# A decoder layer in fp32 on one core: first tiles on two DMA queues, a TensorE start on the identity, and work moved between ScalarE, VectorE and GpSimd

## The chip, the core and the metric

The kernel runs on one core of one Trainium2 chip. The metric is device time in microseconds. The core has five engines that run beside each other and wait for each other on semaphores: TensorE (PE in the profile; its weight loads are PEld), VectorE (DVE), ScalarE (ACT), GpSimd (POOL) and SyncE (SP, which here only issues DMAs). Each engine works its own list of instructions in order.

## The reference

16 sequences of 256 rows with 256 columns go through one layer, all in fp32. Cut to what is computed:

```python
# 1: four heads over 256 fixed keys and values (w_fc, w_proj)
n = layernorm(x) * ln_g + ln_b
p = square(relu(n_heads @ k.T))            # heads of 64, no softmax
x = layernorm(x + (x + p @ v))
# 2: cross attention with 16 heads of 16 on ctx, biased by clipped differences
D = clip(frac[:, None, :] - frac[:, :, None], -0.2, 0.2)
a = gamma * (Q @ K.T) / 4 + delta * (ap * max(D, 0) + an * min(D, 0))
x = layernorm(x + softmax(a) @ V @ Wo.T + bo)
# 3: feed-forward, 1024 wide; each row takes the low-rank addition of one of 8 experts
e = argmax(x @ gate_W.T + gate_b)
x = layernorm(x + relu(x @ wi.T + wi_b + lora(x, e)) @ wo.T + wo_b)
```

## The kernel before

The 4096 rows are 8 blocks of 512 (four tiles of 128 rows) for steps 1 and 3, and 16 batches of 256 for step 2. The order of every engine's work is written out by hand; nothing is scheduled by a planner.

**Loading and the first block (L261 to L307, L896 to L901).** The four tiles of block 0 are loaded by four DMAs on SP (L263), each 128 x 256, and those of later blocks by one DMA each (L260). ln_g and ln_b (L70) and then vv, the values of step 1 (L84), are issued on ACT's queue, with a load of ACT's function tables between them (L78). The keys kT follow the tiles on SP (L83), then block 1, and, from the first slot of the loop, the weights of step 2 (L113). Block 0 is measured by VectorE (L189, L190, one tile after the other), its inverse deviation is made by ACT and VectorE (L198 to L209), and the normed rows xn by ACT (tiles 0 and 1, L249) and VectorE (tiles 2 and 3, L287). TensorE turns them with transposes against an identity (L295), ACT and VectorE evict the two halves (L299, L304).

**Stage 1 (L916 to L994)** is a loop over blocks with eight slots each. In a slot TensorE makes two scores (L314, into one of two PSUM buffers ps_a), ACT takes their Relu (L322), VectorE squares it (L324), and TensorE multiplies the previous slot's squares with vv (L334), into two banks, one of them tagged W. Everything else, such as the next block's norm, is hung into fixed slots.

**Stage 2 with 3 (L1014 to L1148)** is a loop over n = 0 to 65. Step n works on group n: four of the sixteen heads of batch n // 4. In each step TensorE makes the logits of group n (L609) on top of a positive bias that ACT has put into the four banks ps_l (`positive`, L600). The negative bias of the next group is made ahead: `negative(count)` (L582) lets POOL make `count` of its four parts (L588) and ACT the rest (L593). VectorE adds it and takes the row maxima (L624), and the maxima are subtracted for half of the heads by POOL and for half by VectorE (L639). The group before is turned by transposes (`turned`, L649), ACT takes the exponentials (L656), and the one before that is multiplied with the values (`attend`, L665). A "large piece" of another batch hangs in each step (`pieces`, L687): for n a multiple of 4 it is the next batch's queries (`queries`, L433; four products, L437, evicted with scale and bias by ACT, L447).

The feed-forward of a block lies in eight steps, counted by `tb, part = divmod(n - 15, 8)`: part 0 turns its rows (L749), part 1 makes the gates (L764, evicted by ACT, L772), part 2 routes (L777 to L809) and makes the first half of the inner product, part 3 the second half (`inner`, L817; `lora`, L838), and parts 4 to 7 the outer product of one tile each (`finish`, L876, with L860). So n = 16, 24, 32, 40, 48 and 56 have both queries and gates.

All these pieces take PSUM banks from `tile_b` (L49), which hands out three banks in turn: two of psB and the one tagged W. `tile_v` hands out one more, tagged V, which `attend` uses.

The last block of stage 1 (`rest`) has its second norm in stage 2: measured in n = 16 to 19, its scale made in n = 20, its four tiles scaled by ACT and given their bias by POOL (`norm_out`, L376 to L379) at the ends of n = 24, 25, 26 and 27 (L1141). They are batches 14 and 15.

**The end (L1150 to L1187)** finishes the last batch and the feed-forward of blocks 6 and 7. Block 6 makes its first inner half in the four banks ps_l, `lora(0)` evicts them, and its second half goes into the same four banks.

Of the kernel before, what the change touches and what calls it, by code (L numbers as in the profile page):

```python
# [9 lines left out]
FP = mybir.dt.float32  # L10
AF = mybir.ActivationFunctionType
ALU = mybir.AluOpType
AX = mybir.AxisListType

P = 128
EPS = 1e-5
CLAMP = 0.2
BIG = 3.0e38

# [2 lines left out]
def tile_decoder_layer(ctx: ExitStack, tc: tile.TileContext, a: dict, out: bass.AP):  # L22


    nc = tc.nc
    NTOK, C = a["x"].shape
    B, S = a["frac"].shape
    NT = NTOK // P
    NB = NTOK // 512
    CC = C // P  # L30
# [9 lines left out]
    const = ctx.enter_context(tc.tile_pool(name="const", bufs=1))  # L40
# [8 lines left out]
    def tile_b():  # L49

        if turns:
            turns[0] += 1
            if turns[0] % 3 == 0:
                return psV.tile([P, 512], FP, tag="W", name="ps_b")
        return psB.tile([P, 512], FP, tag="B", name="ps_b")

    def tile_v(tag="V"):
        return psV.tile([P, 512], FP, tag=tag, name="ps_v")


    ident = const.tile([P, P], FP, name="ident")
# [3 lines left out]
    rev = const.tile([P, 4, E], FP, name="rev")  # L65
    for e in range(E):
        nc.gpsimd.memset(rev[:, :, e : e + 1], float(E - e))
    def columns(name, src, eng):
        t = const.tile([P, src.shape[1]], FP, name=name)
        eng.dma_start(out=t, in_=src)  # L70
        return t


    kT = const.tile([P, 4, C], FP, name="kT")
    ln_g = columns("ln_g", a["ln_g"], nc.scalar)
    ln_b = columns("ln_b", a["ln_b"], nc.scalar)

    nc.scalar.preload_act_table_set("natural_log_exp_and_others")  # L78
    vv = const.tile([P, CC, C], FP, name="vv")

    def load_first():
        for h in range(2):
            nc.sync.dma_start(out=kT[64 * h : 64 * h + 64], in_=a["kT"])  # L83
        nc.scalar.dma_start(out=vv, in_=a["vv"].rearrange("(c p) f -> p c f", p=P))  # L84


    W = E + ER
    wq, wk, wv, wo = (const.tile([P, CC, C], FP, name=n) for n in ("wq", "wk", "wv", "wo"))
# [8 lines left out]
    bq_s = const.tile([P, CC], FP, name="bq_s")  # L97
# [4 lines left out]
    gamma, delta, qscale = (const.tile([P, 1], FP, name=n) for n in ("gamma", "delta", "qscale"))  # L102
    fcol, nfcol = (const.tile([P, NT], FP, name=n) for n in ("fcol", "nfcol"))
    wib = const.tile([P, FC], FP, name="wib")
# [4 lines left out]

    def load_cross():  # L110
        load = nc.sync.dma_start
        for t, n in ((wk, "wkT"), (wv, "wvT"), (wq, "wqT")):
            load(out=t, in_=a[n].rearrange("(c p) f -> p c f", p=P))  # L113
        for t, n in ((bq, "bq"), (bk, "bk"), (fcol, "frac_cols")):
            load(out=t, in_=a[n])
        for t, n in (
            (bo, "bo"), (apos, "alpha_pos"), (aneg, "alpha_neg"), (gamma, "gamma"),
            (delta, "delta"),
        ):
            load(out=t, in_=a[n].to_broadcast(list(t.shape)))  # L120

        wo_view = a["woT"].rearrange("(o g i d) f -> i g d o f", o=CC, g=4, i=2)
        bv_view = a["bv"].rearrange("x (o g i d) -> i g d (x o)", o=CC, g=4, i=2)
        for i in range(2):
            for g in range(4):
                rows = slice(64 * i + 16 * g, 64 * i + 16 * g + 16)
                load(out=wo[rows], in_=wo_view[i, g])
                load(out=bvc[rows], in_=bv_view[i, g])
# [107 lines left out]
    if True:  # L236
# [16 lines left out]
        class Block:  # L253
# [3 lines left out]
            def load(self):  # L257
                self.x = tile_x()
                if self.tb:
                    nc.sync.dma_start(out=self.x, in_=x_view[self.tb])  # L260
                else:  # L261
                    for j in range(4):
                        nc.sync.dma_start(out=self.x[:, j, :], in_=x_view[0, :, j, :])  # L263

            def measure(self, jj):
                for j in range(2 * jj, 2 * jj + 2):
# [120 lines left out]
    if True:  # L387
# [8 lines left out]
        class Batch:  # L396
# [33 lines left out]
                self.xT = p2.tile([P, CC, S], FP, tag="xT", bufs=1, name="xT")  # L430
                nc.scalar.copy(self.xT.rearrange("p c t -> p (c t)"), ps)

            def queries(self):  # L433
                ps = tile_b()
                for o in range(CC):
                    for c in range(CC):
                        nc.tensor.matmul(  # L437
                            ps[:, o * S : (o + 1) * S],
                            lhsT=wq[:, c, o * P : (o + 1) * P],
                            rhs=self.xT[:, c, :],  # L440
                            start=(c == 0),
                            stop=(c == CC - 1),
                        )
                yield
                self.qT = p2.tile([P, CC, S], FP, tag="qT", name="qT")
                for o in range(CC):
                    nc.scalar.activation(  # L447
                        self.qT[:, o, :], ps[:, o * S : (o + 1) * S], AF.Identity,
                        bias=bq_s[:, o : o + 1], scale=qscale,
                    )  # L450
# [236 lines left out]
        def pieces(n):  # L687

            b, og = divmod(n, 4)
            ahead, nxt, last, older = (  # L690
                batches[b + d] if 0 <= b + d < B else None for d in (2, 1, -1, -2)
            )
            if og == 0:
                return nxt and nxt.queries(), None, []
            later = nxt if nxt and nxt.b >= MADE else None
            if og == 1:
                return older and older.project(), None, [later and (lambda: later.clip("dneg"))]
            if og == 2:
                return nxt and nxt.keys(), None, [later and (lambda: later.clip("dpos"))]
            more = [ahead and ahead.load]  # L700
            if ahead:
                more.append(ahead.reload if ahead.b < MADE else ahead.fractions)
            return nxt and nxt.vals(), ahead and ahead.turned(), more
# [7 lines left out]
    if True:  # L711
        out_view = out.rearrange("(b j p) c -> b p j c", j=4, p=P)

        class Block:
# [99 lines left out]
                self.umT = pm.tile([P, 512], FP, tag="umT", bufs=1, name="umT")  # L814
                nc.scalar.copy(self.umT, ps)

            def inner(self, half, gs=range(4)):  # L817
                if half == 0 and 0 in gs:
                    if self.tb == NB - 1:
                        h0 = pm.tile([P, 4, 512], FP, tag="pT", name="hT0")  # L820
                        h1 = p2.tile([P, 4, 2, S], FP, tag="neg", bufs=3, name="hT1")
                        self.hT = [h0[:, g] for g in range(4)]
                        self.hT += [h1[:, g].rearrange("p j k -> p (j k)") for g in range(4)]
                    else:
                        h = pm.tile([P, FC, 512], FP, tag="hT", bufs=1, name="hT")
                        self.hT = [h[:, f] for f in range(FC)]
                for g in gs:
                    f = 4 * half + g
                    for c in range(CC):
                        nc.tensor.matmul(  # L830
                            banks[g],
                            lhsT=wi[:, c, f * P : (f + 1) * P],
                            rhs=self.xT[:, c, :],
                            start=(c == 0),
                            stop=False,
                        )

            def lora(self, half, scalar=(0, 2)):  # L838
                for g in range(4):
                    f = 4 * half + g  # L840
                    rows = slice(ER * g, ER * g + ER)
                    nc.tensor.matmul(  # L842
                        banks[g], lhsT=loraB[rows, f * P : (f + 1) * P], rhs=self.umT[rows, :],
                        start=False, stop=True,
                    )
                for g in range(4):
                    f = 4 * half + g
                    if g in scalar:
                        nc.scalar.activation(  # L849
                            self.hT[f], banks[g], AF.Relu, bias=wib[:, f : f + 1]  # L850
                        )
                    else:
                        nc.vector.tensor_scalar(  # L853
                            self.hT[f], banks[g], wib[:, f : f + 1], 0.0, ALU.add, ALU.max
                        )

            def outer(self, j, ps):
# [15 lines left out]
                nc.vector.tensor_tensor(rows, rows, ps[:, 0:C], ALU.add)  # L873
                row_stats(rows, self.mv[:, j, :])

            def finish(self, j):  # L876
                ps = tile_b()
                self.outer(j, ps)
                self.add(j, ps)

# [14 lines left out]
    with tc.manual_schedule():  # L895
        rows_in[0].load()  # L896
        load_first()
        rows_in[1].load()
        rows_in[0].begin()
        rows_in[0].turn_in(0)  # L900
        rows_in[0].turn_in(1)  # L901
# [106 lines left out]


        FUSED, FIRST = NB - 2, 15  # L1010
        six, seven = rows_out[NB - 2 :]
        rest = rows_in[NB - 1]
        rest.mv = const.tile([P, 4, 2], FP, name="mv_rest")
        for n in range(N + 2):  # L1014
# [22 lines left out]
            if older and not halved and n != N:  # L1037
                older.attend()
            if nxt:
                nxt.negative(4 if 1 <= n < FIRST - 1 else 3)  # L1040
            if prep:
                prep.root()
            if done:
# [94 lines left out]
                    extra()  # L1138
            if 16 <= n < 20:
                row_stats(rest.y[:, n - 16, :], rest.mv[:, n - 16, :])  # L1140
            if 24 <= n < 28:  # L1141
                rest.norm_out(by[NB], n - 24, n - 24, nc.gpsimd)

            tb, part = divmod(n - FIRST + 4, 8)
            if part < 3 and 0 <= tb <= FUSED:
# [13 lines left out]
        six.inner(0, range(3, 4))  # L1159
        six.lora(0)  # L1160
        end.divide()
        six.inner(1)
        step(add)
        step(add)
        six.lora(1)
        for j in range(2, 4):
            seven.measure(j)
        seven.norm()
        six.finish(0)
        six.finish(1)  # L1170
        seven.turn()
        seven.biased()
# [88 lines left out]
```

## Time and profile before

| | us |
|---|---|
| median of 3 runs (lowest, highest) | 914.95 (913.76, 915.36) |
| the profiled execution | 914.93 |
| its span | 913.1 |
| TensorE busy in the span | 892.4 |
| VectorE busy | 707.7 |
| ScalarE busy | 584.2 |
| GpSimd busy | 379.5 |

The span goes from the first instruction of the program to the last; what lies around it is in the execution's own time. Times in the profile count from the span's start. A row of the timeline gives start, length, engine, line, operation, output and inputs, shape and how many instructions were merged; in brackets stands the engine's idle time ahead of it and what ended that. Matmuls are pipelined, so a row's length holds the last one's way through the array: the distance of two rows' starts is the pace. One fp32 product of the program is two instructions of the trace, a transpose is one.

### The profile page before, as it was taken

The page shows a single profiled execution, that of the slowest core. Times are in us where ns is not written, and L with a number is a line of the kernel's source. Part 1 is how long each engine was busy: PE and PEld are TensorE (multiplying, and loading weights), DVE is VectorE, ACT ScalarE, POOL GpSimd, SP SyncE. Part 2 cuts the span into 40 slices and gives each one's busy share as a digit, 9 for nine tenths or more (in the row PEclk, how much of TensorE's full clock was granted, in tenths as well). Part 3 has the DMA queues.
Part 4 walks back from the last instruction along what each step waited for, and adds up shares of the span by engine and source line. Part 5 has one row for each costly group of instructions (what it writes and reads, how often), then busy time and mean ns, then how long its engine had stood idle before and what let it go on. Part 6 is the DMA issues. An engine that isn't in the chain of part 4 may idle for free.

```text
span 913.1 us, 19025 instructions
## 1 busy us (share of the span) xinstructions
PE 892.4 (98%) x6910; PEld 541.6 (59%) x6910; DVE 707.7 (78%) x1968; ACT 584.2 (64%) x977; POOL 379.5 (42%) x369
## 2 busy tenths in 40 slices
PE   6999999999999999999999999999999999999997
PEld 2333333333356776577658757865875686586555
DVE  5788899889878998778777877777787787678443
ACT  4757877787687879466666856665685567556111
POOL 1002312231469996434635543463454336244010
PEclk9999999999999999999999999999999999999999
DMA  5411011100001222010111202011120201111001
GB/s 137 146 36 35 30 36 41 65 1 2 3 11 50 70 71 56 13 42 21 35 43 39 52 13 66 18 37 41 40 52 14 65 17 40 41 27 45 23 1 47
DMA packets 44190, 37.01 MB, mean 41 GB/s; under 512 B 14912, under 2 KB 40000, under 8 KB 44096
## 3 DMA queue, kind: packets, MB, share of 16 engines
q1 hardware_dynamic: 43536, 35.52, 14.0%
q8 instruction: 55, 0.90, 0.4%
q14 instruction: 39, 0.32, 0.1%
q10 hardware_dynamic: 560, 0.26, 0.1%
HBM read 21.07 MB, written 6.03 MB: 30 GB/s over the span
## 4 chain that ended last, share of the span: by engine, by line
PE 56%; ACT 4%; DVE 1%; issue 1%; ACTq 0%; DVEq 0%
PE ps_b L860 12%; PE ps_l L830 12%; PE ps_b L649 9%; PE ps_l L609 6%; PE ps_v L665 5%; PE ps_b L561 3%; PE ps_b L457 2%; PE ps_b L479 2%; PE ps_l L842 2%; ACT ps_l L600 2%; ACT pT L656 1%; PE ps_b L437 1%; PE ps_b L749 1%; ACT qT L447 1%; DVE neg L624 1%
## 5 line engine op out<-in xcount | busy, mean ns | idle before, releaser
L588 POOL TENSOR_SCALAR neg<-dneg,aneg,delta 128x512 f32<-128x512 f32 x205 | 175.7, 869 | 211.2 <-ACT pT L656 185.8
L624 DVE CUSTOM_DVE_ANT_0 neg<-ps_l,neg 128x256 f32<-128x256 f32 x512 | 181.6, 420 | 43.0 <-PE ps_l L609 39.8
L600 ACT ACTIVATE ps_l<-dpos,apos_d 128x512 f32<-128x512 f32 x256 | 173.1, 686 | 34.5 <-DVE mx L624 30.5
L656 ACT ACTIVATE pT<-ps_b 128x512 f32<-128x512 f32 x256 | 143.3, 590 | 59.1 <-PE ps_b L649 57.4
L324 DVE TENSOR_TENSOR pr<-r 128x1024 f32<-128x1024 f32 x128 | 155.5, 1255 | 32.4 <-ACT r L322 32.1
L322 ACT ACTIVATE r<-ps_a 128x1024 f32<-128x1024 f32 x128 | 126.5, 1022 | 59.1 <-PE ps_a L314 33.9
L649 PE MATMUL ps_b<-ident,neg 128*128 128x128 f32 x1024 | 140.3, 278 | 4.0 <-ACT pT L656 2.4
L649 PEld LDWEIGHTS ps_b<-ident,neg 128*128 128x128 f32 x1024 | 112.9, 140 | 41.9 <-issue 15.3
L639 POOL TENSOR_TENSOR neg<-neg,mx 128x1024 f32<-128x1024 f32 x65 | 124.3, 1914 | 30.0 <-DVE mx L624 24.0
L314 PE MATMUL ps_a<-xnT,kT 64*64 64x512 f32 x1024 | 124.2, 601 | 0.0
L334 PE MATMUL ps_v<-pr,vv 64*64 64x512 f32 x1024 | 123.5, 593 | 0.3
L860 PE MATMUL ps_b<-wof,hT 128*128 128x256 f32 x512 | 115.8, 380 | 0.0
L830 PE MATMUL ps_l<-xt,wi 128*128 128x512 f32 x256 | 115.0, 596 | 0.8 <-ACT hT L849 0.8
L860 PEld LDWEIGHTS ps_b<-wof,hT 128*128 128x128 f32 x512 | 96.4, 190 | 16.0 <-issue 2.3
L639 DVE TENSOR_TENSOR neg<-neg,mx 128x1024 f32<-128x1024 f32 x63 | 90.9, 1443 | 0.3
L349 POOL TENSOR_TENSOR xt<-xt,half 128x512 f32<-128x512 f32 x15 | 23.7, 1583 | 141.0 <-ACT half L348 141.0
L334 PEld LDWEIGHTS ps_v<-pr,vv 64*64 64x64 f32 x1024 | 38.1, 132 | 70.7 <-issue 43.7
L314 PEld LDWEIGHTS ps_a<-xnT,kT 64*64 64x64 f32 x1024 | 38.1, 135 | 67.9 <-issue 56.2
L830 PEld LDWEIGHTS ps_l<-xt,wi 128*128 128x128 f32 x256 | 46.8, 190 | 52.0 <-issue 45.8
L609 PE MATMUL ps_l<-kM,qT 32*128 32x256 f32 x1024 | 74.8, 401 | 0.4 <-ACT ps_l L600 0.4
L665 PE MATMUL ps_v<-pT,vaug 128*32 128x256 f32 x1024 | 69.8, 385 | 0.8 <-ACT pT L656 0.8
L853 DVE TENSOR_SCALAR hT<-ps_l,wib 128x512 f32<-128x512 f32 x44 | 30.5, 745 | 42.8 <-PE ps_l L842 42.8
(107 smaller groups left out, 966.9 us busy)
## 6 DMA issues: line engine op xcount, KB each, us to landing
cT<-in_ctxT SPq DMA_DIRECT2D x16, 256.0 KB
kM<-keys SPq DMA_DIRECT2D x128, 32.0 KB
v<-raw SPq DMA_DIRECT2D x128, 32.0 KB
invs<-rows SPq DMA_DIRECT2D x128, 32.0 KB
x<-in_x SPq DMA_DIRECT2D x7, 512.0 KB
out<-x SPq DMA_DIRECT2D x7, 512.0 KB
frow<-in_frac SPq DMA_DIRECT2D x16, 128.0 KB
wi<-in_wiT SPq DMA_DIRECT2D x1, 1024.0 KB
```

Of the source, the lines that this page charges most:

```text
L314: nc.tensor.matmul(sc[64 * k : 64 * k + 64, h, :], lhsT=kT[64 * h : 64 * h + 64, q, hf * P + 64 * k : hf * P + 64 * k + 64], rhs=self.xnT[ ...
L324: nc.vector.tensor_tensor(pr, r, r, ALU.mult)
L334: nc.tensor.matmul(self.acc[k][64 * h : 64 * h + 64, :], lhsT=vv[64 * k : 64 * k + 64, hf, 64 * q : 64 * q + 64], rhs=pr[64 * k : 64 * k + ...
L588: nc.gpsimd.tensor_scalar(self.neg[:, g], self.batch.dneg, aneg[:, h : h + 1], delta, ALU.mult, ALU.mult,)
L600: nc.scalar.activation(banks[g], self.batch.dpos.rearrange("p j k -> p (j k)"), AF.Copy, scale=apos_d[:, h : h + 1],)
L609: nc.tensor.matmul(banks[g][:, j * S : (j + 1) * S], lhsT=self.batch.qT[rows, self.o, j * P : (j + 1) * P], rhs=self.batch.kM[rows, self.i ...
L624: nc.vector.tensor_tensor_reduce(out=self.t[:, g, j, :], in0=banks[g][:, j * S : (j + 1) * S], in1=self.neg[:, g, j, :], scale=1.0, scalar ...
L639: eng.tensor_tensor(rows, rows, top.to_broadcast([P, 4, S]), ALU.subtract)
L649: nc.tensor.transpose(ps[:, k * S + j * P : k * S + (j + 1) * P], self.t[:, g, j, k * P : (k + 1) * P], ident,)
L656: nc.scalar.activation(self.pT[:, g, :], self.ps[g], AF.Exp)
L830: nc.tensor.matmul(banks[g], lhsT=wi[:, c, f * P : (f + 1) * P], rhs=self.xT[:, c, :], start=(c == 0), stop=False,)
L860: nc.tensor.matmul(ps[:, 0:C], lhsT=self.hT[f][:, j * P : (j + 1) * P], rhs=wof[:, f, :], start=(f == 0), stop=(f == FC - 1),)
```

## The change

- **Start.** Tiles 1 and 3 of block 0 are loaded on ACT's queue, 0 and 2 stay on SP. ln_g, ln_b and the table load come behind them on ACT. vv moves from ACT's queue to SP, behind kT and block 1 and ahead of the weights of step 2. TensorE's list now begins with 30 transposes of the identity against itself into the bank tagged W, ahead of the transposes of block 0; nobody reads their result.
- **Gate steps.** In n = 16, 24, 32, 40, 48 and 56 the two evictions of the queries are done by VectorE (a tensor_scalar with the same scale and bias) and not by ACT. On VectorE they stand between the maxima and the division of an older batch.
- **Negatives.** In parts 0 and 1 of a feed-forward POOL makes all four parts of the negative bias, and ACT none.
- **Last rows.** The four tiles of the last block are scaled at the ends of n = 27, 28, 29 and 35.
- **The end.** Parts 0 and 1 of block 6's second inner half go to banks of `tile_b`, and its first `finish` takes the bank tagged V.

```diff
+WARM = 30
...
     def load_first():
+        for t, n in ((ln_g, "ln_g"), (ln_b, "ln_b")):
+            nc.scalar.dma_start(out=t, in_=a[n])
+        nc.scalar.preload_act_table_set("natural_log_exp_and_others")
         for h in range(2):
             nc.sync.dma_start(out=kT[64 * h : 64 * h + 64], in_=a["kT"])
-        nc.scalar.dma_start(out=vv, in_=a["vv"].rearrange("(c p) f -> p c f", p=P))
...
-        for t, n in ((wk, "wkT"), (wv, "wvT"), (wq, "wqT")):
+        for t, n in ((vv, "vv"), (wk, "wkT"), (wv, "wvT"), (wq, "wqT")):
...
                     for j in range(4):
-                        nc.sync.dma_start(out=self.x[:, j, :], in_=x_view[0, :, j, :])
+                        eng = nc.scalar if j % 2 else nc.sync
+                        eng.dma_start(out=self.x[:, j, :], in_=x_view[0, :, j, :])
...
-            def queries(self):
+            def queries(self, vector=False):
...
                 for o in range(CC):
+                    if vector:
+                        nc.vector.tensor_scalar(
+                            self.qT[:, o, :], ps[:, o * S : (o + 1) * S], qscale,
+                            bq_s[:, o : o + 1], ALU.mult, ALU.add,
+                        )
+                        continue
...
-                return nxt and nxt.queries(), None, []
+                return nxt and nxt.queries(n > 15 and n % 8 == 0), None, []
...
-            def inner(self, half, gs=range(4)):
+            def inner(self, half, gs=range(4), own=()):
+                if 0 in gs:
+                    self.banks = list(banks)
...
+                    if g in own:
+                        self.banks[g] = tile_b()
...
-            def finish(self, j):
-                ps = tile_b()
+            def finish(self, j, ps=None):
+                ps = ps or tile_b()
...
         rows_in[1].load()
+        idle = tile_v("W")
+        for j in range(WARM):
+            nc.tensor.transpose(idle[:, j % 4 * P : (j % 4 + 1) * P], ident, ident)
         rows_in[0].begin()
...
+        LATE = 27, 28, 29, 35
...
-                nxt.negative(4 if 1 <= n < FIRST - 1 else 3)
+                nxt.negative(4 if 1 <= n < FIRST - 1 or (ff and part < 2) else 3)
...
-            if 24 <= n < 28:
-                rest.norm_out(by[NB], n - 24, n - 24, nc.gpsimd)
+            if n in LATE:
+                j = LATE.index(n)
+                rest.norm_out(by[NB], j, j, nc.gpsimd)
...
-        six.inner(1)
+        six.inner(1, own=(0, 1))
...
-        six.finish(0)
+        six.finish(0, tile_v())
```

More of the change, by code (lines that the diff above doesn't have):

```diff
@@ L67, in tile_decoder_layer @@
         nc.gpsimd.memset(rev[:, :, e : e + 1], float(E - e))
[L68 to L71, printed above, removed]
     kT = const.tile([P, 4, C], FP, name="kT")
-    ln_g = columns("ln_g", a["ln_g"], nc.scalar)
-    ln_b = columns("ln_b", a["ln_b"], nc.scalar)
-    nc.scalar.preload_act_table_set("natural_log_exp_and_others")
+    ln_g, ln_b = (const.tile([P, CC], FP, name=n) for n in ("ln_g", "ln_b"))
     vv = const.tile([P, CC, C], FP, name="vv")
     def load_first():
+        for t, n in ((ln_g, "ln_g"), (ln_b, "ln_b")):
+            nc.scalar.dma_start(out=t, in_=a[n])
+        nc.scalar.preload_act_table_set("natural_log_exp_and_others")
         for h in range(2):
             nc.sync.dma_start(out=kT[64 * h : 64 * h + 64], in_=a["kT"])
-        nc.scalar.dma_start(out=vv, in_=a["vv"].rearrange("(c p) f -> p c f", p=P))
     W = E + ER
@@ L828, in inner @@
                     f = 4 * half + g
+                    if g in own:
+                        self.banks[g] = tile_b()
                     for c in range(CC):
                         nc.tensor.matmul(
-                            banks[g],
+                            self.banks[g],
                             lhsT=wi[:, c, f * P : (f + 1) * P],
@@ L842, in lora @@
                     nc.tensor.matmul(
-                        banks[g], lhsT=loraB[rows, f * P : (f + 1) * P], rhs=self.umT[rows, :],
+                        self.banks[g], lhsT=loraB[rows, f * P : (f + 1) * P], rhs=self.umT[rows, :],
                         start=False, stop=True,
@@ L849, in lora @@
                         nc.scalar.activation(
-                            self.hT[f], banks[g], AF.Relu, bias=wib[:, f : f + 1]
+                            self.hT[f], self.banks[g], AF.Relu, bias=wib[:, f : f + 1]
                         )
@@ L853, in lora @@
                         nc.vector.tensor_scalar(
-                            self.hT[f], banks[g], wib[:, f : f + 1], 0.0, ALU.add, ALU.max
+                            self.hT[f], self.banks[g], wib[:, f : f + 1], 0.0, ALU.add, ALU.max
                         )
```

## The prediction

> **What bounds the kernel now.** First the page's busy table, the clock row and the chain of work that ended last.
>
> ```profile
> span 913.1 us, 19025 instructions
> ...
> PE 892.4 (98%) x6910; PEld 541.6 (59%) x6910; DVE 707.7 (78%) x1968; ACT 584.2 (64%) x977; POOL 379.5 (42%) x369
> ...
> PEclk9999999999999999999999999999999999999999
> ...
> PE 56%; ACT 4%; DVE 1%; issue 1%; ACTq 0%; DVEq 0%
> ```
>
> TensorE (PE) is busy for 98% of the span and the chain runs mostly through it, so a gain exists only where PE is idle or runs slowly: 913.1 - 892.4 = 20.7 us idle, of which 8.6 lie ahead of its first matmul and 5.3 behind its last (the last L860 ends at 907.81). The view of waits, for PE alone, tells who ended the larger ones:
>
> ```profile
> PE ps_b L295 <- ACT xn L249: 8.6, 1, 8.6
> PE ps_b L649 <- ACT pT L656: 2.4, 6, 0.5
> PE ps_b L649 <- ACT qT L447: 1.4, 6, 0.2
> PE ps_l L830 <- ACT hT L849: 0.8, 1, 0.8
> PE ps_b L809 <- DVE um L799: 0.5, 1, 0.5
> ```
>
> The first, third, fourth and fifth are places that the change edits. The timeline then tells what each is worth. The start (start, length, engine, line, count):
>
> ```profile
> 5.76 0.43 DVE L189 BATCH_NORM_STATS2 st<-x 128x6 f32<-128x256 f32 x1 [0.22 <-DMA x<-in_x]
> ...
> 8.60 2.15 PE L295 MATMUL ps_b<-ident,xn 128*128 128x128 f32 x8 [8.60 <-ACT xn L249]
> ...
> 10.77 5.93 PE L314 MATMUL ps_a<-xnT,kT 64*64 64x512 f32 x32
> ...
> 18.23 1.90 PE L314 MATMUL ps_a<-xnT,kT 64*64 64x512 f32 x16
> ```
>
> Sixteen L314 take 1.90 us at 18.23, but the first 32 take 5.93. In the single rows, groups of four L314 start 0.86 us apart (10.77, 11.68, 12.53, 13.39) and 0.43 apart from 15.61 on; the group of 15.09 lasts 0.52, which puts the change of pace near 15.27. The transposes do the same: L295 start 0.21 apart here, eight L649 take 1.04 (0.11 apart) later. The clock row says 9 throughout, so it doesn't show this; the pace does.
>
> A gate step, n = 24, its end and step 25; in the second fence the end stage:
>
> ```profile
> 444.56 1.01 ACT L447 ACTIVATE qT<-ps_b,bq_s,qscale 128x256 f32<-128x256 f32 x2
> 444.74 0.66 PE L649 MATMUL ps_b<-ident,neg 128*128 128x128 f32 x4
> ...
> 445.63 0.66 PE L649 MATMUL ps_b<-ident,neg 128*128 128x128 f32 x4 [0.23 <-ACT qT L447]
> ...
> 446.81 0.59 ACT L249 ACTIVATE hid<-y,nm,rs 128x256 f32<-128x256 f32 x1
> ...
> 447.48 0.73 POOL L379 TENSOR_TENSOR hid<-hid,bo 128x256 f32<-128x256 f32 x1 [3.78 <-PE ps_l L609]
> ...
> 448.20 2.26 POOL L588 TENSOR_SCALAR neg<-dneg,aneg,delta 128x512 f32<-128x512 f32 x3
> ...
> 450.71 1.66 DVE L791 TENSOR_TENSOR hot<-lg,top 128x32 f32<-128x32 f32 x1
> ...
> 454.21 0.83 PE L809 MATMUL ps_b<-ident,um 128*128 128x128 f32 x4 [0.45 <-DVE um L799]
> ```
>
> ```profile
> 851.04 7.13 PE L830 MATMUL ps_l<-xt,wi 128*128 128x512 f32 x16 [0.76 <-ACT hT L849]
> ```
>
> Here the reader is to see: a second set of four transposes 0.89 behind the first where 0.44 is the pace; a row that POOL adds ahead of its negatives, with a slow VectorE and a waiting L809 behind it; and one bank wait at the end.
>
> **Start: rows on two queues, keys behind them.** VectorE's statistics begin at 2.97 and end at 6.40, with waits of 0.76 and 0.22 for tiles 2 and 3. The change issues tiles 1 and 3 on ACT at the slots of ln_g and ln_b (0.73, 1.17) instead of on SP at 1.17 and 2.10, and vv (256 KB, issued 1.68, in flight beside tiles 2 and 3) leaves that stretch. It removes at most 0.98 and at least nothing. I take 1.0, since all four tiles are then issued by 1.6: xn of tiles 0 and 1 would be ready at 7.6 and 8.0, not 8.57 and 9.0. Moved past on the queues: ln_g and ln_b start 0.9 later on ACT (needed by the eviction at 9.94, covered by over 5 us), and the table load with them (1.65 to about 2.5, done before 4; Ln is at 6.51). On SP, kT comes 0.9 earlier; wk and all behind it gain 0.9 and lose 0.5 to vv. vv, issued near 3.0, is needed after 13; without that cover each us late is one us. *A page's view:* the Trainium skill, "DMA: Bandwidth & Descriptors", section "Issuing engines are not separate DMA queues", says that a second issuing engine saves only issue time; by that alone tile 3 gains its 0.93 of issue, close to the same sum.
>
> **Start: thirty transposes of the identity.** They need only ident (POOL, done 2.44), so PE begins near 2.55 instead of 8.57. All at the slow pace they last 30 x 0.214 = 6.4, to 9.0. If the clock rises on the way they end sooner. The trace gives two distances to its rise at 15.27: 6.7 us from PE's first weight load (8.57), 4.5 from the first L314 (10.77). With 6.7 the rise is at 9.25 and PE is free at 9.0; with 4.5 it is at 7.05, 21 transposes are slow and 9 take 1.0, and PE is free at 8.05. From a start S at full pace: four transposes 0.44, 0.25 to the eviction, 0.78 eviction, so scores at S+1.5; two groups a score (0.86), 0.2, then Relu 1.02 frees the first of two banks at S+3.6; the second Relu ends at S+4.65; the fourth score ends at S+5.6 and values begin. Before, values began at 16.52. S = 9.0 gives 14.6 (gain 1.9), S = 8.05 gives 13.65 (gain 2.9). I take **2.4**, with the earlier rows in it: they are worth little unless PE is free. From there on PE is continuous for the whole first stage, so nothing gives it back.
>
> *A rule that speaks against it.* The row first: eight transposes from 8.57 to 10.55, L314 without a gap from 10.77, and the pace changes only near 15.27; the trace has no stretch of transposes alone that is long enough to show whether they raise it. The Trainium skill, "TensorE: Matmul & The Clock Gate", Part 4, says that transposes don't count as busy for the clock gate as matmuls do. If so, the warm-up is 6.4 us of nothing and the time is that of the cold rival below. Part 1 of the same page has a free-running window of about 3.4 us; with transposes counted, a rise after one to two windows would lie near 7.65 and the gain, by that, at an estimated 2.6.
>
> **Gate steps (n = 16, 24, 32, 40, 48, 56).** Turned(3) needs the bank that holds the queries; ACT frees it only at 445.57, behind a positive. The loss is 0.89 - 0.44 = 0.45 at each of six. On VectorE: maxima end at 443.03, L437 at 443.72 (+0.2), two evictions at 0.48 (the keys' eviction, L467, median of 32), so free by 444.9; PE wants it at 445.18. Gain 6 x 0.45 = **2.7**, bounds 0 and 3.2 (if the tail of the step goes too). VectorE waits about 0.9 for L437. Queued behind it: divide, half a subtract (both not read until late in step 25), then the next maxima. That queue moves from an end of 445.38 to 444.9 + 0.68 + 1.21 = 446.8; the maxima are due at 447.50 - 0.45 = 447.05, so 0.25 spare. In step 16 the row statistics (0.6) use this up: 0 to 0.35 lost once.
>
> **A fourth negative on POOL in parts 0 and 1**: 0.76 more on POOL, 0.73 less on ACT. In step 24 POOL's three end at 440.98 and the subtract waits 0.83 for maxima, so the fourth fits; the subtract's reader comes 3.6 us later. ACT's next positive waits for maxima anyway (0.18 at 360.64 in step 16). Value 0, bounds -0.3 and +0.3.
>
> **Last rows to n = 27, 28, 29, 35.** In step 25 three POOL negatives start at 448.20, 2.0 behind L609; in step 33 0.3 behind it. VectorE's hot takes 1.66 instead of 0.35 (step 17), and PE loses 0.62 + 0.23 around L809 (twelve L830 in 5.77 where 5.16 is the pace of the other periods, four L809 in 0.67 where it is 0.44). Gain **0.85**. At the new places ACT has 0.8 idle before L600 (415.26) for 0.59, POOL 4.63 before its negatives for 0.73; cost 0, bound 0.4.
>
> **Free banks at the end.** Two of four first L830 groups go to banks free since 848.1 (the um copy). The other two start 3.4 us later, behind the releases by ACT (851.57) and VectorE (851.75). Gain **0.75**, bounds 0 and 0.8. Next late is oT (855.75), wanted at 857.4.
>
> **Sum.** 2.4 + 2.7 + 0.85 + 0.75 = 6.7. The profiled execution took 914.93 (span 913.1 and 1.8 around it; the median is 914.95), so **908.2**.
>
> **Rivals.** *Cold* (the change doesn't warm): PE is free at 9.0, eviction at 10.1 against 9.94, start +0.2 instead of -2.4: 914.93 + 0.2 - 4.3 = **910.8**. For: two us of transposes and the first 4.5 us of L314 did not change the pace; against: the rise is 6.7 us behind the first transpose too, and the trace can't tell the two countings apart. *No gain at the gates*: VectorE's evictions take twice 0.48, freeing the bank at 445.8, as late as ACT: **910.9**. *Slower*: at the six gates VectorE becomes the bound. Divide at its slow 1.30 and subtract at its slow 2.44 (335.06, beside POOL) end at 448.6, 1.6 behind the due maxima; logits, route and L809 follow: 6 x 1.6 = 9.6 lost, 917.8. It decides from 1.4 a step ((6.7 + 1.8) / 6). Against it: POOL's subtract ends at 443.70, so nobody collides. *Both cold and no gain at the gates*: 913.5.
>
> **How the numbers follow.** Forecast 0.58 (own range 907.2 to 909.4), cold 0.27, no gain at the gates 0.07, both 0.05, slower 0.03. Range 906.5 to 911.8: the low end adds the upper bounds at start and gates, the high end takes in cold and its uncertain rise by 1 us. A measurement tells about 0.2% (1.83 us) from no change: faster 0.92, same 0.05, slower 0.03.
>
> **What would show it.** L314's groups 0.43 apart from their first; values (L334) near 14.1; L649's second set 0.44 behind the first at all gates; no wait before L809 in step 25 or L830 at 850. Wrong if L314 starts 0.86 apart behind the transposes, or if maxima at a step n = 17, 25, ... wait for VectorE instead of L609.

## The result and the profile after

| | before | after |
|---|---|---|
| median, us (lowest, highest) | 914.37 (913.76, 915.36), 6 runs | 908.47 (908.11, 908.67), 6 runs |
| ratio after / before, 95% | | 0.9934 [0.9921, 0.9947] |
| the profiled execution, us | 914.93 | 908.42 |
| its span, us | 913.1 | 906.6 |

The change makes the kernel faster by 5.9 us in the medians and by 6.5 us in the two profiled executions; the forecast was 908.2. In the changed kernel lines have moved: L295 is now L292, L314 L311, L334 L331, L649 L652, L656 L659, L609 L612, L600 L603, L447 L450, L830 L838, L809 L812, and VectorE's eviction of queries is L445.

The page of the changed kernel: the busy table and the shares of the chain (the clock row reads 9 in every slice, as before).

```profile
span 906.6 us, 19065 instructions
...
PE 893.8 (99%) x6940; PEld 546.4 (60%) x6940; DVE 708.8 (78%) x1980; ACT 572.2 (63%) x953; POOL 390.2 (43%) x381
...
PE 61%; DVE 0%; ACT 0%; issue 0%; DVEq 0%
```

PE is busy 1.4 us more, with thirty more instructions, and the span is 6.5 us shorter: 12.8 us of idle are left of 20.7. ACT and DVE, 4% and 1% of the chain before, stand at 0% each. TensorE's view of waits:

```profile
PE ps_b L652 <- ACT pT L659: 2.6, 6, 0.5
PE ps_v L910 <- POOL ident masks.py:199: 2.5, 1, 2.5
PE ps_v L668 <- ACT pT L659: 0.8, 1, 0.8
```

Of the four waits that the change edits, xn (8.6), qT (1.4), hT (0.8) and um (0.5), none is left among the larger ones. The first and the third row stand in the first fifteen steps of stage 2 (267 to 350), which the change leaves alone (the first row was 2.4 before); the experiments come back to them. The second is the identity itself. The start, from the timeline:

```profile
2.49 6.19 PE L910 MATMUL ps_v<-ident 128*128 128x128 f32 x30 [2.49 <-POOL ident masks.py:199]
3.40 0.43 DVE L185 BATCH_NORM_STATS2 st<-x 128x6 f32<-128x256 f32 x1 [3.40 <-DMA x<-in_x]
7.08 1.09 ACT L245 ACTIVATE xn<-x,nm,rs 128x256 f32<-128x256 f32 x2 [0.82 <-DVE nm L240]
8.52 1.04 PE L292 MATMUL ps_b<-ident,xn 128*128 128x128 f32 x8
9.99 1.95 PE L311 MATMUL ps_a<-xnT,kT 64*64 64x512 f32 x16 [0.43 <-ACT xnT L296]
14.05 1.90 PE L331 MATMUL ps_v<-pr,vv 64*64 64x512 f32 x16
```

Eight transposes of the block last 1.04 us instead of 2.15, sixteen L311 1.95, and the values begin at 14.05 instead of 16.52. In the single rows the transposes of the identity start 0.21 apart up to 8.08 and 0.11 apart after it: the pace rose during transposes alone, 5.6 us behind PE's start. The gate step n = 24:

```profile
441.07 1.00 DVE L445 TENSOR_SCALAR qT<-ps_b,qscale,bq_s 128x256 f32<-128x256 f32 x2 [0.80 <-PE ps_b L434]
441.98 1.09 PE L652 MATMUL ps_b<-ident,neg 128*128 128x128 f32 x8
...
444.30 0.42 DVE L627 CUSTOM_DVE_ANT_0 neg<-ps_l,neg 128x256 f32<-128x256 f32 x1 [0.49 <-PE ps_l L612]
...
445.91 1.90 POOL L642 TENSOR_TENSOR neg<-neg,mx 128x1024 f32<-128x1024 f32 x1
...
447.50 0.35 DVE L794 TENSOR_TENSOR hot<-lg,top 128x32 f32<-128x32 f32 x1
...
450.38 0.60 PE L812 MATMUL ps_b<-ident,um 128*128 128x128 f32 x4
```

The eight transposes are one row again, where two sets of four stood 0.89 apart. VectorE still waits 0.49 for the logits ahead of its maxima, so its longer queue is not yet late. In step 25, POOL's subtract comes sooner, hot takes 0.35 instead of 1.66, and L812 starts without a wait. And the end stage:

```profile
844.51 3.70 PE L838 MATMUL ps_b<-xt,wi 128*128 128x512 f32 x8
```

Eight L838 go into new banks without a wait, and the other eight follow at 848.05, without one too.

**Where the 6.5 us came from.** PE works the same list in both kernels, apart from the thirty transposes, so each instruction can be laid beside itself. The shift is by how much sooner an instruction starts in the changed kernel; it grows where something was gained and shrinks where something was lost:

| place | shift gained, us |
|---|---|
| start, up to the values (16.52 to 14.05) | 2.47 |
| six gate steps (0.44 to 0.46 each) | 2.70 |
| step 25, at L838 and L812 | 0.85 |
| end, at L838 | 0.83 |
| small ones: lost near 288 (0.28), 427 (0.14) and 518 (0.16), gained near 437 (0.26) | -0.33 |
| sum | 6.52 |

### The profile page after: what moved, and what is told of

Same layout as the page of the kernel before. It is cut to its first block, busy times and chain, and to the rows that moved or that the text cites. A ratio compares the mean times of both kernels' runs of the same rounds, so it can differ in the third digit from the quotient of the medians.

```text
span 906.6 us, 19065 instructions
## 1 busy us (share of the span) xinstructions
PE 893.8 (99%) x6940; PEld 546.4 (60%) x6940; DVE 708.8 (78%) x1980; ACT 572.2 (63%) x953; POOL 390.2 (43%) x381
## 4 chain that ended last, share of the span: by engine, by line
PE 61%; DVE 0%; ACT 0%; issue 0%; DVEq 0%
PE ps_l L838 12%; PE ps_b L868 12%; PE ps_b L652 11%; PE ps_v L668 6%; PE ps_l L612 6%; PE ps_b L564 3%; PE ps_b L482 2%; PE ps_b L460 2%; PE ps_b L434 2%; PE ps_l L850 2%; PE ps_b L767 1%; PE ps_b L752 1%; PE ps_b L421 1%; PE ps_v L868 0%; PE ps_b L838 0%; PE ps_b L812 0%
## 5 line engine op out<-in xcount | busy, mean ns | idle before, releaser
L591 POOL TENSOR_SCALAR neg<-dneg,aneg,delta 128x512 f32<-128x512 f32 x217 | 187.3, 875 | 209.6 <-PE ps_b L652 123.2
L603 ACT ACTIVATE ps_l<-dpos,apos_d 128x512 f32<-128x512 f32 x256 | 173.2, 686 | 41.1 <-DVE mx L627 37.7
L659 ACT ACTIVATE pT<-ps_b 128x512 f32<-128x512 f32 x256 | 142.6, 590 | 60.5 <-PE ps_b L652 58.8
L652 PE MATMUL ps_b<-ident,neg 128*128 128x128 f32 x1024 | 139.1, 278 | 2.8 <-ACT pT L659 2.6
L652 PEld LDWEIGHTS ps_b<-ident,neg 128*128 128x128 f32 x1024 | 113.0, 140 | 39.4 <-issue 16.9
L331 PE MATMUL ps_v<-pr,vv 64*64 64x512 f32 x1024 | 123.5, 593 | 0.3
L311 PE MATMUL ps_a<-xnT,kT 64*64 64x512 f32 x1024 | 122.2, 592 | 0.7 <-ACT xnT L296 0.4
L868 PE MATMUL ps_b<-wof,hT 128*128 128x256 f32 x496 | 112.3, 380 | 0.0
L838 PE MATMUL ps_l<-xt,wi 128*128 128x512 f32 x248 | 111.5, 595 | 0.0
L868 PEld LDWEIGHTS ps_b<-wof,hT 128*128 128x128 f32 x496 | 93.4, 190 | 15.0 <-issue 1.5
L642 DVE TENSOR_TENSOR neg<-neg,mx 128x1024 f32<-128x1024 f32 x63 | 92.8, 1473 | 0.3
L331 PEld LDWEIGHTS ps_v<-pr,vv 64*64 64x64 f32 x1024 | 38.1, 132 | 70.7 <-issue 43.2
L311 PEld LDWEIGHTS ps_a<-xnT,kT 64*64 64x64 f32 x1024 | 37.6, 133 | 67.0 <-issue 55.5
L612 PE MATMUL ps_l<-kM,qT 32*128 32x256 f32 x1024 | 74.8, 401 | 0.4 <-ACT ps_l L603 0.4
L838 PEld LDWEIGHTS ps_l<-xt,wi 128*128 128x128 f32 x248 | 45.3, 190 | 49.0 <-issue 44.6
L668 PE MATMUL ps_v<-pT,vaug 128*32 128x256 f32 x1024 | 69.8, 385 | 0.8 <-ACT pT L659 0.8
```

The costliest lines, as they stand in the source:

```text
L311: nc.tensor.matmul(sc[64 * k : 64 * k + 64, h, :], lhsT=kT[64 * h : 64 * h + 64, q, hf * P + 64 * k : hf * P + 64 * k + 64], rhs=self.xnT[ ...
L331: nc.tensor.matmul(self.acc[k][64 * h : 64 * h + 64, :], lhsT=vv[64 * k : 64 * k + 64, hf, 64 * q : 64 * q + 64], rhs=pr[64 * k : 64 * k + ...
L591: nc.gpsimd.tensor_scalar(self.neg[:, g], self.batch.dneg, aneg[:, h : h + 1], delta, ALU.mult, ALU.mult,)
L603: nc.scalar.activation(banks[g], self.batch.dpos.rearrange("p j k -> p (j k)"), AF.Copy, scale=apos_d[:, h : h + 1],)
L612: nc.tensor.matmul(banks[g][:, j * S : (j + 1) * S], lhsT=self.batch.qT[rows, self.o, j * P : (j + 1) * P], rhs=self.batch.kM[rows, self.i ...
L642: eng.tensor_tensor(rows, rows, top.to_broadcast([P, 4, S]), ALU.subtract)
```

## The experiments

Each kernel differs from the changed one by the diff shown, but for warm_alone, which is built on the kernel before. The kernel before was timed again beside three groups of these runs, with medians of 914.77, 914.72 and 914.44; ratios are to those.

| kernel | median, us (lowest, highest) | ratio to before, 95% | against 908.47 |
|---|---|---|---|
| no_warm | 909.98 (909.63, 910.20) | 0.9948 [0.9936, 0.9961] | +1.51 |
| gate_act | 910.91 (910.49, 911.08) | 0.9957 [0.9943, 0.9971] | +2.44 |
| neg_three | 908.46 (908.01, 908.61) | 0.9931 [0.9919, 0.9944] | -0.01 |
| late_early | 909.15 (908.59, 909.35) | 0.9939 [0.9926, 0.9951] | +0.68 |
| end_shared | 909.25 (908.76, 909.47) | 0.9937 [0.9925, 0.9950] | +0.78 |
| one_queue | 908.40 (907.52, 908.56) | 0.9926 [0.9913, 0.9938] | -0.07 |
| warm_16 | 909.47 (908.83, 909.82) | 0.9939 [0.9925, 0.9953] | +1.00 |
| warm_alone | 912.97 (912.67, 913.29) | 0.9981 [0.9972, 0.9989] | +4.50 |
| gate_load | 915.54 (915.39, 916.03) | 1.0014 [1.0005, 1.0023] | +7.07 |
| exps_first | 907.61 (907.38, 907.78) | 0.9925 [0.9913, 0.9937] | -0.86 |
| rows_behind | 906.90 (906.79, 907.18) | 0.9918 [0.9904, 0.9931] | -1.57 |
| both | 906.40 (906.19, 906.86) | 0.9913 [0.9899, 0.9927] | -2.07 |

The last column compares medians of different groups, and the kernel before differed by 0.4 us between groups, so a difference under some 0.4 us in it says nothing by itself; where one matters, the shift of PE's instructions is given too. A shift between two profiles holds the start's own variation: in the nine profiles with both the split and thirty transposes the pace rises between 6.2 and 8.2 and values begin between 13.52 and 14.18.

**no_warm: the thirty transposes taken out.**

```
-WARM = 30
+WARM = 0
```

> The changed kernel without the 30 transposes of the identity, all else kept. Theory (transposes alone raise TensorE's pace, and the slow first 6 us of before were the price of a late start): the block's transposes begin when xn is ready, near 8.2, at 0.21 apart, L311's first groups are 0.86 apart again, and values begin some 1.9 to 2.6 later than at 14.05; about 910.4 to 911. Rival (the time since launch or the loads decide the pace, and the transposes only stand in the way): L311 at 0.43 from the start and 908.1 to 908.5.

PE's rows of the start:

```profile
10.02 4.23 PE L311 MATMUL ps_a<-xnT,kT 64*64 64x512 f32 x24
...
15.45 1.90 PE L331 MATMUL ps_v<-pr,vv 64*64 64x512 f32 x16
```

The eight L292 ahead of them (from 7.84) are 0.21 apart, L311 goes in groups 0.86 apart until about 12.9, and values begin 1.40 later than with the warm-up. The transposes do raise the pace, and the sign is as the theory had it. The size is less than forecast (909.98, not 910.4 to 911), because the pace also rises sooner by itself: 5.1 us behind PE's first instruction here, 6.7 in the kernel before.

**warm_alone: the warm-up put into the kernel before, nothing else.**

```
+        idle = tile_v("W")
+        for j in range(30):
+            nc.tensor.transpose(idle[:, j % 4 * P : (j % 4 + 1) * P], ident, ident)
         rows_in[0].begin()
```

> The kernel before with the 30 transposes of the identity added and nothing else changed. Theory (the pace is the larger part of the start's gain): block 0's tiles 0 and 1 are ready at 8.6 and 9.0, all transposes and L314 run at full pace, values begin at 14.6 to 14.9, so 1.6 to 1.9 below before. Rival (the gain needs the earlier rows): under 0.8.

Values begin at 14.57, 1.95 ahead of the kernel before, and 1.75 of that arrives in the median. As expected. Here xn is the later one: PE has finished the thirty at 7.7 and waits 0.89 for it. So the rest of the start's 2.47, some 0.52, is what earlier rows are worth between these two profiles, both at the higher pace; against all nine with both parts of the change it is 0.39 to 1.05.

**warm_16: fewer transposes.**

```
-WARM = 30
+WARM = 16
```

> The changed kernel with 16 transposes of the identity instead of 30: TensorE is busy from 2.5 to 5.9 and idle to 8.2. Theory (the pace rises only after a stretch of unbroken work, seen as 5.5 us with transposes alone and 6.7 in before): the pace is not yet full at 8.2, L311 begins at 0.86 apart and the time lies 1 to 2 us above 908.5. Rival (a few us of work suffice and a break does no harm): block 0 turns from 8.2 at full pace, 908.1.

```profile
8.05 0.34 PE L292 MATMUL ps_b<-ident,xn 128*128 128x128 f32 x1 [1.88 <-ACT xn L245]
8.54 0.98 PE L292 MATMUL ps_b<-ident,xn 128*128 128x128 f32 x7 [0.16 <-ACT xn L245]
9.96 4.24 PE L311 MATMUL ps_a<-xnT,kT 64*64 64x512 f32 x24 [0.43 <-ACT xnT L296]
```

PE's rows behind the sixteen. The granted clock of the same run, asked for by stretch (stretch, its length, PE's busy time and instructions, clock, the DMA engines' share and GB/s):

```profile
6.10:9.40 3.30, 1.26 (x9) 1.00 1.05 319
9.50:12.90 3.40, 2.97 (x17) 0.50 0.73 199
```

The reader is to see two changes of pace. The sixteen (2.49 to 5.75) start 0.21 apart, yet those of the block, at 8.54, start 0.11 apart: the pace had risen, where the theory had it still low. L311 from 9.96 is back at 0.86, until 12.9: it was lost again, and there the granted clock reads 0.50. Ahead of that lies a stretch in which PE was busy for 1.26 of 3.30 us and started nothing for 2.3 us (5.75 to 8.05). The time is the theory's (1.00 above 908.47), but its reason was wrong, and of the rival only the block's transposes at full pace came true: a break does harm. In warm_alone PE stood idle for 0.89 (7.7 to 8.6) and the pace stayed; where between the two the limit lies, no run shows. At this start the transposes had to reach not only to the rise but close to the block's own.

**one_queue: all four first tiles on SP, as before; the keys still behind them.**

```
-                        eng = nc.scalar if j % 2 else nc.sync
+                        eng = nc.sync
```

> The changed kernel with all four first tiles on SyncE's queue; vv stays behind the keys, and the thirty transposes stay. Theory (the tiles come sooner by issue time, but TensorE is busy with the identity until 8.5 and xn is ready at 8.2): the split is worth only what reaches beyond 8.5, 0.3 to 0.6, so 908.8 to 909.1. Rival (the whole 0.8 between 8.17 and 9.0 counts): 909.3.

```profile
2.88 0.43 DVE L185 BATCH_NORM_STATS2 st<-x 128x6 f32<-128x256 f32 x1 [2.88 <-DMA x<-in_x]
...
6.71 1.09 ACT L245 ACTIVATE xn<-x,nm,rs 128x256 f32<-128x256 f32 x2 [0.82 <-DVE nm L240]
```

A miss for theory and rival alike: the time is the same. On one queue the first tile landed 0.52 sooner than on two (2.88 against 3.40), the last statistics began at 4.64 against 5.01, and xn was ready 0.37 sooner. The first tile's delay is more than chance: the first statistics begin at 3.22 to 3.88 in all eleven profiles with the split and at 2.85 to 2.97 in the three without. What brought the last tiles in sooner than in the kernel before is that vv, the one load of that stretch that differs, no longer moves beside them: the last statistics began at 5.76 and 5.86 with vv there (before, warm_alone). In this profile PE hides what the one queue gained: the pace rose only at 8.6, PE was in its thirty transposes until 8.7, and values began at 14.31. That the split gains nothing is what the times show.

**gate_act: ACT evicts the queries again.**

```
-                return nxt and nxt.queries(n > 15 and n % 8 == 0), None, []
+                return nxt and nxt.queries(), None, []
```

> The changed kernel with the queries evicted by ScalarE at all gate steps, as before; the fourth negative stays on GpSimd. Theory (the bank is freed too late behind a positive): the second set of four transposes starts 0.89 behind the first again at six steps, 6 x 0.45 = 2.7, 911.2. Rival (ScalarE's load was the cause, and the negative that left it has already cured that): less than 1 us, below 909.5.

The timeline of step n = 24:

```profile
442.24 0.66 PE L652 MATMUL ps_b<-ident,neg 128*128 128x128 f32 x4
443.12 0.65 PE L652 MATMUL ps_b<-ident,neg 128*128 128x128 f32 x4 [0.23 <-ACT qT L450]
```

The two sets stand 0.88 apart again, PE's wait for qT is back at 1.4 us in six, and the shift is 2.48: 0.43 to 0.45 at each gate, less 0.14 that comes back at 425, where the change had one of its small losses.

**gate_load: how much more VectorE bears at the gates.** Behind its evictions it gets two products of a tile that nothing reads any more; this is work added, and nothing depends on it.

```
+                        if o:
+                            for r in range(2):
+                                nc.vector.tensor_tensor(self.xT, self.xT, self.xT, ALU.mult)
```

> The changed kernel with two more VectorE operations (a product of 128x512 on a tile that is no longer read, 0.68 us each) behind the queries' evictions at the six gate steps. They compute nothing that is used. Theory (VectorE has 0.49 us of spare time before its next maxima at five gates and none at the first): 1.36 - 0.49 = 0.87 late at five, 1.36 at one, and the routing passes it on, some 4.5 to 5.7 more, 913 to 914. Rival (routing and logits have cover of their own): under 1.5 us, below 910.

The added pair, POOL's subtract behind the maxima, and the routing of step 25:

```profile
443.60 1.41 DVE L451 TENSOR_TENSOR xT<-xT 128x512 f32<-128x512 f32 x2
...
448.69 1.89 POOL L645 TENSOR_TENSOR neg<-neg,mx 128x1024 f32<-128x1024 f32 x1
...
449.86 0.77 DVE L797 TENSOR_TENSOR hot<-lg,top 128x32 f32<-128x32 f32 x1
```

The load is 1.41 us a gate and 0.49 of it had cover, which leaves 0.92. By the shift a gate cost 1.1 to 1.2, and the first one, which has no cover, 1.7. At n = 24, 0.75 of it is lost where the inner product (L841) waits for the late maxima (3.5 us in six in TensorE's view of waits, a row that the changed kernel does not have), and some 0.5 further on in the same feed-forward. The direction was forecast rightly and the size too small (4.5 to 5.7 against 7.07). The kernel is then no faster than before the change, so the rival that VectorE becomes the bound has a real mechanism; the change stops half a microsecond short of it at five gates, and with nothing to spare at the first.

**neg_three: the fourth negative given back to ACT.**

```
-                nxt.negative(4 if 1 <= n < FIRST - 1 or (ff and part < 2) else 3)
+                nxt.negative(4 if 1 <= n < FIRST - 1 else 3)
```

> The changed kernel with three negatives on GpSimd and one on ScalarE in parts 0 and 1, as before. Theory (both engines have spare time there): no difference, 908.2 to 908.8. Rival (ScalarE's relief is part of the gain at the gates): 0.2 to 0.45 at each of six steps, 909.7 to 911.

No difference. This part of the change could be left out.

**late_early: the last rows back at their old steps.**

```
-        LATE = 27, 28, 29, 35
+        LATE = 24, 25, 26, 27
```

> The changed kernel with the last block's rows at the ends of n = 24 to 27, as before. Theory: GpSimd's add ahead of its negatives at the end of n = 24 delays the routing of step 25, L812 waits again, 0.85 more, 909.3. Rival (the gate's earlier end gives GpSimd the time): under 0.3.

In step 25, POOL's subtract and VectorE's hot:

```profile
447.42 1.89 POOL L642 TENSOR_TENSOR neg<-neg,mx 128x1024 f32<-128x1024 f32 x1
...
447.65 1.70 DVE L794 TENSOR_TENSOR hot<-lg,top 128x32 f32<-128x32 f32 x1
```

hot is not slow work: it ends at 449.35, 0.04 behind the subtract's 449.31. The late row on POOL moves the subtract on to hot, and hot stands until the subtract is done. L812 then waits 0.49 for um again. The shift grows by 0.89 there, and 0.16 comes back at 514, where the change had another of its small losses; 0.72 is left at the end.

**end_shared: the last block's second half in the banks that `lora` has to clear.**

```
-        six.inner(1, own=(0, 1))
+        six.inner(1)
...
-        six.finish(0, tile_v())
+        six.finish(0)
```

> The changed kernel with the second inner half of block 6 in the four shared banks and the first finish in a bank of tile_b, as before. Theory: the wait of 0.76 for ScalarE's eviction comes back and reaches the end undiminished, 909.2. Rival (the last batch's DMA, its rows of inverse sums, ends the stage anyway): no difference, 908.5.

PE's wait for hT is back at 0.8 (L838 at 845.30 with 0.76 idle ahead of it), shift 0.83.

**exps_first, rows_behind and both: the waits that are left.** The row of 2.6 in six says that transposes wait for a bank whose exponential stands behind two positives on ACT (steps 2 to 14). The row of 0.8 is one place, step 14, where four norms of rows (L245, 2.07 us) stand ahead of exponentials on ACT.

```
 exps_first, for n < FIRST (15):
-                if nxt:
+                if nxt and n >= FIRST:
                     nxt.positive(2)
...
+                if nxt and n < FIRST:
+                    nxt.positive(2)
 (the second one behind turned(1) and exps(1))
 rows_behind:
-                if prep:
+                if prep and n >= FIRST:
                     prep.rows()
...
+            if prep and n < FIRST:
+                prep.rows()
 (the second one at the end of the step)
```

> The changed kernel with ScalarE's second exponential ahead of its third positive for n < 15. It is the same fault as at the gates: there the second set of transposes waits for a bank that ScalarE frees behind a positive (0.44 idle at 279.62, 0.38 at 267.16, five such places of 0.7 to 0.8 in all). Theory: 0.4 to 0.5 at five places, 906.0 to 906.5. Rival (the third positive becomes late for the next logits): no gain or up to 1 us more.

> The changed kernel with the four scaled rows of block 0's feed-forward (2.1 us of ScalarE in n = 14) behind the step's last exponentials, not ahead. Theory: the 1.86 us that attend (L668) loses at 348 goes, but part comes back in step 15, where the transposes of the rows wait for banks: 0.8 to 1.5 less, 907.0 to 907.7. Rival: all of it comes back in step 15, 908.5.

> Both edits together on the changed kernel. Theory: the two places are apart, so the gains add: 904.6 to 905.9. Rival: step 14 is common to both, and the sum falls short by the larger part of one of them.

exps_first removes the whole row of 2.6 from the view, and gains 0.86 (0.66 by the shift in these steps): a third of what the theory named, and not the loss of the rival. PE's row of logits tells why, with the changed kernel at 287.09 first and exps_first behind it:

```profile
287.09 1.15 PE L612 MATMUL ps_l<-kM,qT 32*128 32x256 f32 x16
```

```profile
286.17 1.73 PE L612 MATMUL ps_l<-kM,qT 32*128 32x256 f32 x16
```

The logits start 0.92 sooner and take 0.58 longer: they now wait, bank by bank, for the positives that were put back. The sum of the waits was not the price, since the next wait stood close behind the first. rows_behind gains 1.57 in the median: the wait of L668 is gone, and the turning of rows has a new one, behind ACT:

```profile
352.74 0.66 PE L752 MATMUL ps_b<-ident,x 128*128 128x128 f32 x4 [0.44 <-ACT pT L659]
```

Of its shift 0.45 was there at the first values (13.60 against 14.05) and belongs to the start. Counted from there it is 1.85 at its peak near 351, and 0.7 of that is given back by 354, so that 1.17 is the edit's own, within the 0.8 to 1.5 named. Together they gain 2.07 in the median, less than the 2.43 of the two sums. By the shift in stage 2 they bring 0.70 and 1.02, against 0.66 and 1.17 apart, so they all but add; the forecast for both was missed because it rested on that for exps_first. That kernel, at 906.40 against 914.44 for the kernel before, is faster than both kernels of this case.

## Why the prediction was right

**The sum.** 6.7 was forecast against the profiled execution, 6.5 came. All four terms were near: start 2.4 (2.47), gates 2.7 (2.70 by the shift, 2.44 when undone), last rows 0.85 (0.85, and 0.68 to 0.72 when undone), end 0.75 (0.83, 0.78). The fourth negative, set at 0, is 0. The terms came to 6.85, and small losses of 0.33 in all were not foreseen. Two of them belong to parts of the change: near 518 the loss is gone when the last rows stand at their old steps (late_early), near 427 when ACT evicts the queries (gate_act). The one near 288 stands behind a gap of 0.28 on ACT between two positives; the eleven kernels with tiles on ACT's queue have that gap and the three without do not. What makes it, no run shows, nor what gained 0.26 near 437. For step 25 the place and the price were right, but the reason behind the slow hot was left unnamed there: it is the overlap with POOL's subtract (late_early).

**The start was right in sum, and one step in it wrong.** The step that failed is the first one: "The change issues tiles 1 and 3 on ACT ... It removes at most 0.98 and at least nothing. I take 1.0". The statistics did not begin at 2.97 but at 3.40, and one_queue, which keeps SP alone, is as fast. The two tiles of xn on ACT ended 0.78 sooner than before (7.68 and 8.17 against 8.46 and 8.95), and by another way: with vv gone and one queue they ended 1.15 sooner, and the split took 0.37 of that back. The second step held: PE was free of the thirty between 8.05 and 9.0, at 8.5, and values came at 14.05 where 14.1 was named. That it came so near is in part luck: the pace rises at a different time in each profile, and the same start gained between 2.3 and 3.0 in nine of them. "They are worth little unless PE is free" held as well: about 0.5 beside the warm-up (warm_alone against the change), 1.07 without it (values at 15.45 in no_warm against 16.52, of which 0.76 is PE's earlier beginning and the rest a pace that rose sooner behind it).

**Cold fell.** It had 0.27, because the trace of before held no long stretch of transposes alone. Eleven runs now have one, and in all eleven the pace had doubled before any matmul ran. The Trainium skill, "TensorE: Matmul & The Clock Gate", Part 4, says that the full clock doesn't engage for transposes; for these fp32 transposes the runs show the contrary, 0.21 to 0.11 us apart with no matmul yet run. Part 1 of the page, a free-running window of about 3.4 us, agrees better: the rise came 3.6 to 6.1 us behind PE's start, at a different point in each run.

**No gain at the gates fell** with gate_act. VectorE's two evictions took 1.00 together and ended at 442.07, and PE came to the second set of four at 442.42 (441.98 and four times 0.11). **Slower** was named with its price and did not come: 0.25 of spare was forecast in a gate step, 0.49 was there in five of six, and none in step 16, as the 0 to 0.35 there said. So one sign of being wrong did come: the maxima of n = 17 follow VectorE's own work and not the logits. But they stand 1.31 behind the logits' start, where 1.30 is the distance at n = 25, and nothing was lost by it. gate_load shows the mechanism at work 0.5 us further on, and at 1.1 to 1.3 us lost for each us beyond the cover it is a little steeper than the one for one that the rival assumed.

## What to carry to other kernels

Price a wait by what stands behind it: the same view of waits showed 1.4 us in six at the gates, worth 2.5, and 2.6 us in six in the steps before, worth 0.7 to 0.9, because in the one nothing else was late and in the other the next wait stood 0.3 behind. When a start is cold, give TensorE work that needs no input and let it run on until the real work is there; measure the pace from start to start, since busy time and the page's clock row don't show it. When several edits are made for one stretch, undo each by itself: here the second queue and the fourth negative were worth nothing, and the sum hid it. Between two profiles, take off what they already differ by ahead of the edit.

## What the runs showed of the hardware

- The pace of TensorE rises in transposes alone: fp32 128 x 128 from 0.21 to 0.11 us apart, at 6.1 to 8.6 in the eleven runs with thirty transposes from 2.49 on. In no_warm, without them, it rose 5.1 us behind PE's first instruction.
- It falls again: a stretch of 2.3 us without a start (warm_16) was followed by block transposes at full pace and then by 2.9 us of matmuls at half pace. The clock row of the page read 9 in every slice all the same. Asked for by stretch, the granted clock of warm_16 is 0.50 from 9.5 to 12.9, but 1.00 from 2.5 to 6.0, where the transposes stand 0.21 apart too: what lies ahead of the first rise it does not show.
- Four tiles of 128 KB on two queues arrived no sooner than on one (statistics from 3.40 to 5.01 against 2.88 to 4.64; the first from 3.22 to 3.88 in eleven profiles against 2.85 to 2.97 in three).
- VectorE's hot, which reads two tiles, never ends before a subtract of POOL that overlaps it: in six blocks of each of the two main kernels, of late_early and of gate_load it ended 0.04 to 0.05 behind the subtract's end, with lengths of 0.35, 0.77, 1.66 and 1.70, and without a subtract beside it (two blocks) it took 0.19. The Trainium skill, "GPSIMD Engine Reference", section "1. Specifications", has the SBUF interfaces of the two shared, with contention for VectorE instructions of two SBUF inputs; the rows agree, and show hot ending only behind the whole subtract, however early in it hot began.
